# Joint product's tile kept for all batches and laid out by output rows; eight stores a batch; scores' half added up by block rows; another order at the end

## The chip, the cores and the metric

One Trainium2 chip, one core of it. The metric is the device time of one execution in microseconds; lower is better. Every time below is from the runs of the kernel before or from the profile of one of its executions. TensorE multiplies into eight accumulator banks, ScalarE and VectorE work on tiles, GpSimd does a few sums and issues the accumulating transfers, SyncE issues the other transfers.

## The reference, cut to what matters

32 graphs of 512 nodes with 512 features each, all in float32, pass through two layers:

```python
# layer 0
h   = max(layernorm(x), 0)
agg = einsum('bij,bjf->bif', adj, h) / max(sum(adj, -1), 1e-6)
x   = x + relu(concat([h, agg]) @ W.T)
# layer 1
h   = max(layernorm(x), 0)
q, k = split(h @ Wqk);  v = h @ Wv
agg = einsum('bij,bjd->bid', adj, k * mask)
w   = mask / sqrt(512) * einsum('bid,bid->bi', q, agg)
out = x + softmax(w, axis=nodes)[:, :, None] * v
```

Each graph ("batch") is independent of the others; the weights are shared.

## The kernel before

**Products.** Every 512x512 product is cut into 2x2 blocks of 256 and done with seven block products in place of eight: sums of blocks of the left and right factor are made beforehand (`left_sums`, `right_sums`: four additions each), and the seven results are added up into the four output blocks. The products run in the order 1, 2, 6, 5, 7, 3, 4 (`ORDER`).

**Layer 1 rewritten.** With M = Wq Wk^T, made once at the start, the row sums of q times agg are the row sums of (h M) times (adj (mask h)). So a batch needs a joint product of h with the pair M and Wv, called `tv` (index 0 of `which` is the scores' half h M, index 1 the values' half h Wv), and a product `u` of adj with mask h. `tv` applies the seven-product scheme twice, once over block rows and once more within: its blocks of 128 lie at seven "places", which must still be added up (`recombine`, seven additions for each half) before they are rows of the result. For each of the outer seven products it fills four banks, numbered n = 0 to 3, of two places each (the last of one), in the order 2, 1, 3, 0. ScalarE copies the banks of products 1, 6, 7 and 4 into the tile (`keep`), VectorE adds those of 2, 3 and 5 (`plus`, and the adds of `m_tv`). Products 1 and 6 continue in the same banks, so product 6 cannot begin before ScalarE has copied product 1's banks away; products 1 and 2 together occupy all eight banks.

**A period.** The main loop runs four stages of TensorE work in each period i, each a generator that is advanced step by step:

- `layer0_out(i)`, 14 steps: the output of layer 0 (`pp_o`, `pr_o`, `pq_o`),
- `layer1_tv(i - 1)`, 14 steps: the joint product (`ptv`),
- `layer1_u(i)`, 7 steps: adj times masked h (`pp_u` ...),
- `layer0_y(i + 1)`, 7 steps: h times the second half of W (`pp_y` ...).

What the other engines do is written out by hand as a `Plan`: `p.at(n, f, ...)` puts call f after step n of the stage. Each engine executes its instructions in that order, so an instruction that waits holds up all that come later on its engine. SyncE's transfers also go out in this order.

**What hangs on the joint product's tile.** In the stage after it VectorE adds up the scores' half, multiplies it by `U` and sums the rows (`dot`), then come the scores, their maximum over all nodes (GpSimd), the exponentials, the sum and the weights `sm`. In `layer0_out` of the following period ScalarE scales the four row groups of the values' half (`apply`, steps 2 to 5), GpSimd adds x to each half of them by an accumulating transfer from a DRAM copy (`add_x1`; the copy was written by `keep` of `FrontH1`), and SyncE stores them to the output (`store`, steps 9, 9, 11, 11: four transfers of 64 KB for each row group, 16 in all). Directly after that stage the next joint product begins, into the next tile of the same tag:

```python
t = big.tile([P, 4, 2, 7, P], F32, tag="tv", bufs=1, name=f"tv_{b}")
```

With one buffer, the first write into the new tile waits until everything that used the old one is done.

**Other names.** `FrontH1.write` normalises the rows of h for layer 1 (`h1m`, with `nmr` and `rstd` from VectorE's statistics) and writes them to DRAM (`dh1T`), from where they are read back in another order (`sh1T`) and turned; `mask` multiplies the same rows in place by the node mask on ScalarE, after that write has landed; `masked_sums` are the sums of `h1m` for `u`. `FrontA` does the same for adj (`a`, `daT`, `saT`), `FrontH` for layer 0's h (`n`, `dhT`, `shT`, `hT` in the tile `wide`). `inner_sums` are the second-level sums of `h1T` for the joint product. Reads of `a` for the batch after next are issued at steps 2 and 3 of the joint product, between the writes `dh1T`.

After the loop the last joint product runs alone (written into `wide`), with the end of batch 30 (`post`) and of batch 31 (`final`) beside and after it.

Of the kernel before, what the change touches and what calls it, by code (L numbers as in the profile page):

```python
# [16 lines left out]
P = 128  # L17
# [5 lines left out]
def kernel(  # L23
# [330 lines left out]
    class FrontH1:  # L354


        def __init__(self, b):
            self.b = b
            self.to = Turned("h1T", b)
            self.t = norm_tiles(f"1_{b}")  # L360
            self.x1 = dram.tile([2, P, 2, 2, H], F32, tag="dx1", name=f"dx1_{b}")
# [4 lines left out]
        def keep(self):  # L366
            for c in range(C):
                nc.sync.dma_start(
                    out=self.x1[c // 2][:, :, c % 2, :], in_=X[self.b][:, c, :].rearrange("p (a f) -> p a f", a=2)
                )  # L370
# [81 lines left out]
    def layer1_tv(b):  # L452


        if b + 1 < B:
            t = big.tile([P, 4, 2, 7, P], F32, tag="tv", bufs=1, name=f"tv_{b}")
        else:
            t = wide.rearrange("p s a (b f) -> p (s a b) f", f=P).rearrange("p (o a i) f -> p o a i f", o=4, a=2)
# [20 lines left out]
        def part(o, n):  # L479
            return t[:, o, :, 2 * n:min(2 * n + 2, 7), :].rearrange("p a b f -> p a (b f)")  # L480
# [29 lines left out]
    class Post:  # L510
# [12 lines left out]
        def recombine(self, i, blocks, which, on=None):  # L523
            def s(j):
                return TV[self.b][:, blocks, which, PLACE[j], :]

            o, x1, x2 = [(2, 1, 2), (1, 1, 6), (5, 1, 5), (3, 5, 3), (6, 1, 7), (7, 5, 7), (4, 6, 4)][i]
            add(s(o), s(x1), s(x2), on)

        def row(self, c, which):  # L530

            r, i = c // 2, c % 2
            return TV[self.b][:, 2 * r:2 * r + 2, which, 2 * i:2 * i + 2, :].rearrange("p a b f -> p a (b f)")

        def dot(self, c):
            v = self.row(c, 0)
            u = U[self.b][:, 2 * (c // 2):2 * (c // 2) + 2, c % 2, :]
            nc.vector.scalar_tensor_tensor(
                v, v, 1.0, u, op0=ALU.mult, op1=ALU.mult, accum_out=self.acc[:, c:c + 1]
            )  # L540
# [25 lines left out]

        def add_x1(self, h):
            nc.gpsimd.dma_start(
                out=TV[self.b][:, 2 * h:2 * h + 2, 1, 0:4, :].rearrange("p a i f -> p a (i f)"),
                in_=self.f1.x1[h].rearrange("p a i f -> p a (i f)"), accum_op=ALU.add,  # L570
            )

        def load_x1(self, h):
            self.n[h] = half_tile(f"x1_{self.b}_{h}")
            nc.sync.dma_start(out=self.n[h], in_=self.f1.x1[h].rearrange("p a i f -> p a (i f)"))

        def finish(self, c):

            x1 = self.n[c // 2].rearrange("p a (i f) -> p a i f", i=2)[:, :, c % 2, :]
            v = self.row(c, 1)  # L580
            nc.vector.scalar_tensor_tensor(v, v, self.sm[:, c:c + 1], x1, op0=ALU.mult, op1=ALU.add)

        def store(self, c):
            v = self.row(c, 1)
            for q, dst in enumerate(by_rows(out[self.b])):
                nc.sync.dma_start(  # L586
                    out=dst[:, c, :].rearrange("r (a f) -> r a f", a=2), in_=v[q * R:(q + 1) * R]
# [4 lines left out]
    w2R, hT = wide[:, 0:7], wide[:, 7:14]  # L592

# [245 lines left out]
    ends, middle, every = slice(0, 4, 3), slice(1, 3), slice(0, 4)  # L839
# [4 lines left out]
    with tc.manual_schedule(engines=engines):  # L844
        weights, mvR = start()
        post = None
        for i in range(B):
            more, last = i + 1 < B, i + 1 == B
            if i > 0:
# [8 lines left out]
                if i == 1:  # L858
# [9 lines left out]
                    p.at(6, FH[3].load, 0)  # L868
                    p.at(8, FH[3].load, 1)
                f1 = F1[i - 1]  # L870
                if post is not None:
                    for k in (5, 6):
                        p.at(0, post.recombine, k, every, 1)
                p.at(0, f1.turn, 0)
                p.at(1, f1.turn, 1)
                if post is not None:
                    for c in range(C):
                        p.at(2 + c, post.apply, c)
                        p.at([9, 9, 11, 11][c], post.store, c)
                    p.at(3, post.add_x1, 0)  # L880
                    p.at(5, post.add_x1, 1)
                for k in range(4):
# [33 lines left out]
                for c in range(C):  # L916
                    p.at([2, 3, 5, 6][c], f.write, c)
                    p.at(7 + c, f.mask, c)
                p.at(6, f.keep)
                for k in range(4):  # L920
                    p.at([9, 11, 12, 12][k], f.masked_sums, k)
# [16 lines left out]
                for k in range(7):  # L938
                    p.at(10 + k // 2, post.recombine, k, ends, 0)
# [16 lines left out]
            elif more:  # L956
                for k in range(7):
                    p.at(k // 4, post.recombine, k, middle, 0)
# [14 lines left out]
            else:  # L973
                p.at(0, f.turn, 0)
                p.at(1, f.turn, 1)
                for k in range(4):
                    p.at(2 + k // 2, f.sums, k)
                for k in range(4):
                    p.at(4 + k // 2, f.inner_sums, k, 0, 7)
# [5 lines left out]
            if more:  # L985
# [6 lines left out]
                if i > 0:  # L992
# [3 lines left out]
                    for k in range(5):  # L996
                        p.at(3 + (k + 1) // 2, post.recombine, k, every, 1)
# [26 lines left out]
        for k in range(7):  # L1024
            p.at(k // 2, post.recombine, k, every, 1, nc.gpsimd)
            p.at(1 + k // 2, post.recombine, k, middle, 0)
# [6 lines left out]
        for n, blocks in ((10, ends), (12, slice(1, 2))):  # L1033
            for k in range(7):
                p.at(n + k // 4, final.recombine, k, blocks, 0)
        p.at(12, post.shift)
        p.at(12, post.exponents)
        p.at(12, post.row_sum)
        p.at(13, post.weights)
# [4 lines left out]
        for k in range(7):  # L1044
            final.recombine(k, slice(2, 3), 0)
# [4 lines left out]
        for c in range(C):  # L1050
            post.apply(c)
        for k in range(3):
            final.recombine(k, every, 1)
# [41 lines left out]
```

## Time and profile before

| | |
|---|---|
| time, median of 3 runs | 2482.16 us (2480.3 to 2483.52) |
| span of the profiled execution | 2479.5 us |
| busy: TensorE, VectorE, ScalarE, GpSimd | 2306.0, 1938.8, 1081.8, 507.0 us |
| transfers | 463.71 MB, 468222 packets, mean 187 GB/s |
| stores to the output | 512 of 64 KB, 2.1 us from issue to landing |
| accumulating transfers | 62 of 512 KB, 8.0 us to landing |
| adds within the joint product's tile, of 128x256 | 0.42 us each (median) |

Busy time is a sum over the span; whether an engine sets the end is seen only from what waits for what, and where. The profile names a group of instructions by line, engine, operation and tile; `tv<-ptv` is a copy from a bank into the joint product's tile. After a number of us for idle time stands what ended it.

### The profile page before, as it was taken

The page shows a single profiled execution, that of the slowest core. Times are in us where ns is not written, and L with a number is a line of the kernel's source. Part 1 is how long each engine was busy: PE and PEld are TensorE (multiplying, and loading weights), DVE is VectorE, ACT ScalarE, POOL GpSimd, SP SyncE. Part 2 cuts the span into 40 slices and gives each one's busy share as a digit, 9 for nine tenths or more (in the row PEclk, how much of TensorE's full clock was granted, in tenths as well). Part 3 has the DMA queues.
Part 4 walks back from the last instruction along what each step waited for, and adds up shares of the span by engine and source line. Part 5 has one row for each costly group of instructions (what it writes and reads, how often), then busy time and mean ns, then how long its engine had stood idle before and what let it go on. Part 6 is the DMA issues. An engine that isn't in the chain of part 4 may idle for free.

```text
span 2479.5 us, 32904 instructions
## 1 busy us (share of the span) xinstructions
PE 2306.0 (93%) x10372; PEld 1997.3 (81%) x10372; DVE 1938.8 (78%) x3622; ACT 1081.8 (44%) x2031; POOL 507.0 (20%) x453
## 2 busy tenths in 40 slices
PE   7999999999999999999999999999999999999983
PEld 6788888887888888888888888888888888888872
DVE  6787778877778878788777788777788777798774
ACT  4354443454443444434444434544434544434331
POOL 0120222211222202222202222112222112222120
PEclk9999999999999999999999999999999999999996
DMA  9867687877787877877776878777877777777542
GB/s 221 230 187 190 176 217 181 201 191 186 192 207 175 208 189 179 210 187 188 200 187 176 218 178 203 194 193 180 218 176 204 192 194 184 207 181 189 129 111 51
DMA packets 468222, 463.71 MB, mean 187 GB/s; under 512 B 43312, under 2 KB 342320, under 8 KB 468048
## 3 DMA queue, kind: packets, MB, share of 16 engines
q1 hardware_dynamic: 451184, 429.10, 66.2%
q0 software_dynamic: 16864, 32.51, 7.5%
q8 instruction: 82, 1.34, 0.2%
q14 instruction: 92, 0.75, 0.1%
HBM read 293.93 MB, written 167.51 MB: 186 GB/s over the span
## 4 chain that ended last, share of the span: by engine, by line
PE 50%; DMA 17%; DVE 12%; SPq 8%; ACT 6%; issue 3%; POOL 3%; ACTq 0%; DVEq 0%; POOLq 0%
PE ptv L469 16%; PE pp_u L130 7%; SPq L586 7%; PE pp_y L130 7%; DMA tv<-dx 6%; PE pp_o L130 6%; DMA out_dram<-tv 4%; PE pq_u L130 4%; DVE tv L94 3%; PE pq_y L130 3%; PE pr_o L130 3%; ACT tv L100 2%; POOL y L97 2%; DVE h1T L97 2%; PE pr_y L130 2%
## 5 line engine op out<-in xcount | busy, mean ns | idle before, releaser
L469 PE MATMUL ptv<-mv,h1T 128*128 128x256 f32 x3136 | 736.7, 397 | 105.8 <-ACT tv L100 97.5
L469 PEld LDWEIGHTS ptv<-mv,h1T 128*128 128x128 f32 x3136 | 622.8, 200 | 214.5 <-ACT tv L100 109.6
L100 ACT ACTIVATE tv<-ptv 128x512 f32<-128x512 f32 x496 | 247.3, 549 | 300.6 <-DMA out_dram<-tv 204.2
L94 DVE TENSOR_TENSOR tv<-tv 128x256 f32<-128x256 f32 (+1 forms) x644 | 314.9, 512 | 8.5
L97 DVE TENSOR_TENSOR h1T<-h1T 128x512 f32<-128x512 f32 (+1 forms) x192 | 258.3, 1358 | 1.2
L130 PE MATMUL pp_u<-h1m,aT 128*128 128x256 f32 x1024 | 242.7, 380 | 8.2 <-DVE h1m L97 8.2
L130 PE MATMUL pp_y<-wide 128*128 128x256 f32 x1024 | 243.2, 381 | 0.0
L130 PE MATMUL pp_o<-y,aT 128*128 128x256 f32 x1024 | 243.1, 380 | 0.0
L130 PE MATMUL pp_o<-w,wide 128*128 128x256 f32 x992 | 236.4, 381 | 4.2 <-DMA w<-dw 4.2
L97 DVE TENSOR_TENSOR h1m<-h1m 128x512 f32<-128x512 f32 x128 | 88.8, 694 | 189.5 <-ACT h1m L382 188.4
L130 PEld LDWEIGHTS pp_u<-h1m,aT 128*128 128x128 f32 x1024 | 193.7, 190 | 38.1 <-issue 6.3
L130 PEld LDWEIGHTS pp_o<-y,aT 128*128 128x128 f32 x1024 | 195.4, 191 | 27.0
L130 PEld LDWEIGHTS pp_y<-wide 128*128 128x128 f32 x1024 | 195.4, 191 | 26.7
L130 PEld LDWEIGHTS pp_o<-w,wide 128*128 128x128 f32 x992 | 189.2, 191 | 31.4 <-issue 5.5
L94 DVE TENSOR_TENSOR tv<-ptv,tv 128x512 f32<-128x512 f32 x248 | 141.7, 612 | 89.6 <-ACT tv L100 69.2
L547 POOL PARTITION_ALL_REDUCE gtop<-top x32 | 22.2, 693 | 923.8 <-DVE top L544 923.8
L97 POOL TENSOR_TENSOR y<-y 128x512 f32<-128x512 f32 x124 | 192.8, 1555 | 16.8 <-DVE y L94 14.4
L100 ACT ACTIVATE o<-pp_o 128x512 f32<-128x512 f32 x96 | 57.3, 597 | 298.7 <-PE pp_o L130 298.7
L248 POOL TENSOR_TENSOR rstd<-rstd,mhalf 128x2 f32<-128x2 f32 (+1 forms) x96 | 78.4, 817 | 499.8 <-DVE rstd L247 499.8
L100 ACT ACTIVATE xu<-pp_u 128x512 f32<-128x512 f32 x128 | 76.4, 597 | 207.9 <-PE pp_u L130 202.3
L258 ACT ACTIVATE n<-n,nmr,rstd 128x512 f32<-128x512 f32 x120 | 88.3, 804 | 165.4 <-DVE nmr L252 144.0
L100 ACT ACTIVATE y<-pp_y 128x512 f32<-128x512 f32 x128 | 76.4, 597 | 169.0 <-PE pp_y L130 169.0
(113 smaller groups left out, 3464.3 us busy)
## 6 DMA issues: line engine op xcount, KB each, us to landing
w<-dw SPq DMA_DIRECT2D x217, 256.0 KB, 4.5
xu<-in_x_dram SPq DMA_DIRECT2D x128, 256.0 KB, 4.5
a<-in_adj_dram SPq DMA_DIRECT2D x256, 128.0 KB, 3.1
dh1T<-h1m SPq DMA_DIRECT2D x128, 256.0 KB, 3.1
dx<-xu SPq DMA_DIRECT2D x128, 256.0 KB, 3.5
sh1T<-dh1T SPq DMA_DIRECT2D x256, 128.0 KB, 4.4
shT<-dhT SPq DMA_DIRECT2D x248, 128.0 KB, 4.2
daT<-a SPq DMA_DIRECT2D x124, 256.0 KB, 4.5
```

Of the source, the lines that this page charges most:

```text
L94: (on or nc.vector).tensor_tensor(o, a, b, op=ALU.add)
L97: (on or nc.vector).tensor_tensor(o, a, b, op=ALU.subtract)
L100: nc.scalar.activation(o, i, AF.Copy)
L130: nc.tensor.matmul(p[:, rc, :], lt[:, LEFT[k], dk, ts(rc, P)], right[:, dk, :], start=first and n == 0, stop=True, skip_group_check=True,)
L248: nc.gpsimd.tensor_tensor(rstd[:, a:b], rstd[:, a:b], mhalf[:, a:b], op=ALU.pow)
L258: nc.scalar.activation(o, i, AF.Relu, scale=t[1][:, c:c + 1], bias=t[2][:, c:c + 1])
L469: nc.tensor.matmul(banks[n][:, :, ts(i, P)], left[:, LEFT[k], LEFT_IN[j], :], mvR[:, RIGHT[k], RIGHT[j], :, :], start=first and i == 0, st ...
L547: nc.gpsimd.partition_all_reduce(self.gtop, self.top, channels=P, reduce_op=ReduceOp.max)
L586: nc.sync.dma_start(out=dst[:, c, :].rearrange("r (a f) -> r a f", a=2), in_=v[q * R:(q + 1) * R])
```

## The change

- The joint product's tile `tv` is allocated once, for all batches, in place of a new tile for each batch under one buffer. Waits then go by the parts of the tile that an instruction touches.
- Its layout becomes [row half, scores or values, 14 positions, 128]: a pair of places of both blocks of a row half lie side by side, so that positions 0 to 7 of a half are its 256 output rows' values in order, and 8 to 13 are places that hold intermediate sums. Which places a bank covers stays.
- The output is stored by halves: 4 transfers for each of two halves, at steps 9 and 11, with 4 KB in a row on the tile's side. `keep` writes x in one transfer in place of four, and the accumulating transfers read and write 4 KB in a row.
- `recombine` takes a row half (0, 1, or both) in place of a list of blocks. The scores' half of row half 0 is added up at steps 12 and 13 (before: blocks 0 and 3 at steps 10 to 13), that of row half 1 at steps 0 and 1 of `u` (before: blocks 1 and 2).
- `mask` moves from steps 7, 8, 9, 10 to 7, 7, 8, 9, `masked_sums` from 9, 11, 12, 12 to 9, 10, 10, 11. In the second period two loads move from steps 6 and 8 to 9 and 10.
- At the end: batch 30's weights, scaling, accumulation and stores move beside the last joint product; the sums of `h1T` for it are made for the first two slots before the rest; the last batch is stored by halves, half of the transfers issued by ScalarE.

```diff
--- before.py
+++ after.py
@@ -358,16 +358,13 @@
             self.b = b
             self.to = Turned("h1T", b)
             self.t = norm_tiles(f"1_{b}")
-            self.x1 = dram.tile([2, P, 2, 2, H], F32, tag="dx1", name=f"dx1_{b}")
+            self.x1 = dram.tile([P, 2048], F32, tag="dx1", name=f"dx1_{b}")
 
...
         def keep(self):
-            for c in range(C):
-                nc.sync.dma_start(
-                    out=self.x1[c // 2][:, :, c % 2, :], in_=X[self.b][:, c, :].rearrange("p (a f) -> p a f", a=2)
-                )
+            nc.sync.dma_start(out=self.x1, in_=X[self.b].rearrange("p c f -> p (c f)"))
 
...
@@ -452,10 +449,11 @@
     def layer1_tv(b):
 
 
+
         if b + 1 < B:
-            t = big.tile([P, 4, 2, 7, P], F32, tag="tv", bufs=1, name=f"tv_{b}")
+            t = tv
         else:
-            t = wide.rearrange("p s a (b f) -> p (s a b) f", f=P).rearrange("p (o a i) f -> p o a i f", o=4, a=2)
+            t = wide.rearrange("p s a (b f) -> p (s a b) f", f=P).rearrange("p (r w i) f -> p r w i f", r=2, w=2)
         TV[b] = t
         left = H1T[b]
 
@@ -477,7 +475,8 @@
                 yield half
 
         def part(o, n):
-            return t[:, o, :, 2 * n:min(2 * n + 2, 7), :].rearrange("p a b f -> p a (b f)")
+            first = [0, 4, 8, 12][n] + (2 if n < 3 else 1) * (o % 2)
+            return t[:, o // 2, :, first:first + min(2, 7 - 2 * n), :].rearrange("p w b f -> p w (b f)")
 
...
@@ -520,20 +519,24 @@
                 setattr(self, n, small.tile([P, 1], F32, tag=n, name=f"{n}_{b}"))
             self.n = {}
 
-        def recombine(self, i, blocks, which, on=None):
+        def recombine(self, i, rows, which, on=None):
+
+
             def s(j):
-                return TV[self.b][:, blocks, which, PLACE[j], :]
+                p = PLACE[j]
+                first, step = (12, 1) if p == 6 else ([0, 4, 8][p // 2] + p % 2, 2)
+                t = TV[self.b][:, :, which, first:first + step + 1:step, :]
+                return t if rows is None else t[:, rows]
 
             o, x1, x2 = [(2, 1, 2), (1, 1, 6), (5, 1, 5), (3, 5, 3), (6, 1, 7), (7, 5, 7), (4, 6, 4)][i]
             add(s(o), s(x1), s(x2), on)
 
         def row(self, c, which):
 
-            r, i = c // 2, c % 2
-            return TV[self.b][:, 2 * r:2 * r + 2, which, 2 * i:2 * i + 2, :].rearrange("p a b f -> p a (b f)")
+            return TV[self.b][:, c // 2, which, 4 * (c % 2):4 * (c % 2) + 4, :].rearrange("p i f -> p (i f)")
 
         def dot(self, c):
-            v = self.row(c, 0)
+            v = self.row(c, 0).rearrange("p (a f) -> p a f", a=2)
             u = U[self.b][:, 2 * (c // 2):2 * (c // 2) + 2, c % 2, :]
             nc.vector.scalar_tensor_tensor(
                 v, v, 1.0, u, op0=ALU.mult, op1=ALU.mult, accum_out=self.acc[:, c:c + 1]
@@ -564,32 +567,35 @@
             v = self.row(c, 1)
             nc.scalar.activation(v, v, AF.Copy, scale=self.sm[:, c:c + 1])
 
+        def half(self, h):
+
+            return TV[self.b][:, h, 1, 0:8, :].rearrange("p i f -> p (i f)")
+
         def add_x1(self, h):
-            nc.gpsimd.dma_start(
-                out=TV[self.b][:, 2 * h:2 * h + 2, 1, 0:4, :].rearrange("p a i f -> p a (i f)"),
-                in_=self.f1.x1[h].rearrange("p a i f -> p a (i f)"), accum_op=ALU.add,
-            )
+            nc.gpsimd.dma_start(out=self.half(h), in_=self.f1.x1[:, ts(h, 1024)], accum_op=ALU.add)
 
         def load_x1(self, h):
             self.n[h] = half_tile(f"x1_{self.b}_{h}")
-            nc.sync.dma_start(out=self.n[h], in_=self.f1.x1[h].rearrange("p a i f -> p a (i f)"))
+            nc.sync.dma_start(out=self.n[h].rearrange("p c f -> p (c f)"), in_=self.f1.x1[:, ts(h, 1024)])
 
         def finish(self, c):
 
-            x1 = self.n[c // 2].rearrange("p a (i f) -> p a i f", i=2)[:, :, c % 2, :]
             v = self.row(c, 1)
-            nc.vector.scalar_tensor_tensor(v, v, self.sm[:, c:c + 1], x1, op0=ALU.mult, op1=ALU.add)
-
-        def store(self, c):
-            v = self.row(c, 1)
+            nc.vector.scalar_tensor_tensor(
+                v, v, self.sm[:, c:c + 1], self.n[c // 2][:, c % 2, :], op0=ALU.mult, op1=ALU.add
+            )
+
+        def store(self, h, also=None):
+            v = self.half(h).rearrange("p (c f) -> p c f", c=2)
             for q, dst in enumerate(by_rows(out[self.b])):
-                nc.sync.dma_start(
-                    out=dst[:, c, :].rearrange("r (a f) -> r a f", a=2), in_=v[q * R:(q + 1) * R]
+                (also if also is not None and q % 2 else nc.sync).dma_start(
+                    out=dst[:, 2 * h:2 * h + 2, :], in_=v[q * R:(q + 1) * R]
                 )
 
 
     wide = const.tile([P, 14, 2, H], F32, name="wide")
     w2R, hT = wide[:, 0:7], wide[:, 7:14]
+    tv = const.tile([P, 2, 2, 14, P], F32, name="tv")
 
     def weight_source(src):
         return src.rearrange("(k r) j -> k r j", r=R)
...
@@ -865,20 +870,21 @@
...
                     FH[3] = FrontH(3)
-                    p.at(6, FH[3].load, 0)
-                    p.at(8, FH[3].load, 1)
+                    p.at(9, FH[3].load, 0)
+                    p.at(10, FH[3].load, 1)
                 f1 = F1[i - 1]
                 if post is not None:
                     for k in (5, 6):
-                        p.at(0, post.recombine, k, every, 1)
+                        p.at(0, post.recombine, k, None, 1)
                 p.at(0, f1.turn, 0)
                 p.at(1, f1.turn, 1)
                 if post is not None:
                     for c in range(C):
                         p.at(2 + c, post.apply, c)
-                        p.at([9, 9, 11, 11][c], post.store, c)
                     p.at(3, post.add_x1, 0)
                     p.at(5, post.add_x1, 1)
+                    p.at(9, post.store, 0)
+                    p.at(11, post.store, 1)
                 for k in range(4):
                     p.at(2 + k, f1.sums, k)
                 for k in range(4):
@@ -915,10 +921,10 @@
                 p.at(3, shift, f.t, 2, 4)
                 for c in range(C):
                     p.at([2, 3, 5, 6][c], f.write, c)
-                    p.at(7 + c, f.mask, c)
+                    p.at([7, 7, 8, 9][c], f.mask, c)
                 p.at(6, f.keep)
                 for k in range(4):
-                    p.at([9, 11, 12, 12][k], f.masked_sums, k)
+                    p.at([9, 10, 10, 11][k], f.masked_sums, k)
                 if i + 2 < B:
                     fa = FA[i + 2] = FrontA(i + 2)
                     p.at(2 if i > 1 else 11, fa.load, 0)
@@ -936,7 +942,7 @@
                 p.at(6, exchanged.to.read, 0)
                 p.at(7, exchanged.to.read, 1)
                 for k in range(7):
-                    p.at(10 + k // 2, post.recombine, k, ends, 0)
+                    p.at(12 + k // 4, post.recombine, k, 0, 0)
                 run(layer1_tv(i - 1), 14, p)
 
 
@@ -955,7 +961,7 @@
                 p.at(3, FA[1].to.read, 1)
             elif more:
                 for k in range(7):
-                    p.at(k // 4, post.recombine, k, middle, 0)
+                    p.at(k // 4, post.recombine, k, 1, 0)
                 for c in range(C):
                     p.at(2 + c // 2, post.dot, c)
                 p.at(4, post.scores)
@@ -972,11 +978,14 @@
                         p.at(5, fa.degrees, 1)
             else:
                 p.at(0, f.turn, 0)
+                for k in range(3):
+                    p.at(1, f.inner_sums, k, 0, 2)
                 p.at(1, f.turn, 1)
                 for k in range(4):
                     p.at(2 + k // 2, f.sums, k)
+                p.at(4, f.inner_sums, 3, 0, 2)
                 for k in range(4):
-                    p.at(4 + k // 2, f.inner_sums, k, 0, 7)
+                    p.at(5 + k // 2, f.inner_sums, k, 2, 7)
             if more:
                 p.at(5, load_x, i + 1)
             run(layer1_u(i), 7, p)
@@ -994,7 +1003,7 @@
                     p.at(2, post.row_sum)
                     p.at(4, post.weights)
                     for k in range(5):
-                        p.at(3 + (k + 1) // 2, post.recombine, k, every, 1)
+                        p.at(3 + (k + 1) // 2, post.recombine, k, None, 1)
                 p.at(2, FA[i].factor)
                 if i == 0:
                     p.at(0, fh.write, 2)
@@ -1022,48 +1031,48 @@
         final = Post(B - 1, F1[B - 1])
         p = Plan()
         for k in range(7):
-            p.at(k // 2, post.recombine, k, every, 1, nc.gpsimd)
-            p.at(1 + k // 2, post.recombine, k, middle, 0)
+            p.at(k // 2, post.recombine, k, None, 1, nc.gpsimd)
+            p.at(1 + k // 2, post.recombine, k, 1, 0)
         for c in range(C):
             p.at(5 + c // 2, post.dot, c)
         p.at(7, post.scores)
         p.at(7, post.maximum)
         p.at(2, final.load_x1, 0)
         p.at(3, final.load_x1, 1)
-        for n, blocks in ((10, ends), (12, slice(1, 2))):
-            for k in range(7):
-                p.at(n + k // 4, final.recombine, k, blocks, 0)
-        p.at(12, post.shift)
-        p.at(12, post.exponents)
-        p.at(12, post.row_sum)
-        p.at(13, post.weights)
+        for k in range(7):
+            p.at(12, final.recombine, k, 0, 0)
+        p.at(8, post.shift)
+        p.at(8, post.exponents)
+        p.at(9, post.row_sum)
+        p.at(10, post.weights)
+        for c in range(C):
+            p.at(10 + c, post.apply, c)
+        p.at(11, post.add_x1, 0)
+        p.at(13, post.add_x1, 1)
+        p.at(13, post.store, 0)
+        p.at(13, post.store, 1)
         p.at(13, final.dot, 0)
         p.at(13, final.dot, 1)
         run(layer1_tv(B - 1), 14, p)
 
         for k in range(7):
-            final.recombine(k, slice(2, 3), 0)
+            final.recombine(k, 1, 0)
         final.dot(2)
         final.dot(3)
         final.scores()
         final.maximum()
-        for c in range(C):
-            post.apply(c)
         for k in range(3):
-            final.recombine(k, every, 1)
+            final.recombine(k, None, 1)
         final.shift()
         final.exponents()
         final.row_sum()
-        for h in range(2):
-            post.add_x1(h)
         for k in range(3, 7):
-            final.recombine(k, every, 1)
+            final.recombine(k, None, 1)
         final.weights()
         for c in range(C):
             final.finish(c)
-            final.store(c)
-        for c in range(C):
-            post.store(c)
+            if c % 2:
+                final.store(c // 2, nc.scalar)
 
 
 # ---- launch: one core; inputs and outputs as the reference has them ----
```

More of the change, by code (lines that the diff above doesn't have):

```diff
@@ L836, in start @@
         return [right_sums(outer)[k] for k in range(4)] + [right_sums(inner)[k] for k in range(4)], mv
-    ends, middle, every = slice(0, 4, 3), slice(1, 3), slice(0, 4)
     engines = {
```

## Prediction

> **What bounds the kernel now.** I read the waits first (who waited for whom, in total over the span), then one batch in the timeline, then stretches of that batch with clock and busy time, then VectorE's timeline, because a second limit must lie behind the first.
>
> ```profile
> ACT tv L100 <- DMA out_dram<-tv: 204.2, 30, 15.3
> ...
> PEld ptv L469 <- ACT tv L100: 109.6, 30, 4.5
> ...
> PE ptv L469 <- ACT tv L100: 97.5, 30, 4.1
> ...
> PE pp_u L130 <- DVE h1m L97: 8.2, 8, 1.5
> ```
>
> TensorE (93% busy) has one large wait: 97.5 us, in 30 of 32 batches, in the joint product, for ScalarE's copies into `tv`; ScalarE in turn waits for stores that read `tv`. One batch shows how:
>
> ```profile
> 1246.10 10.32 SPq L586 DMA_DIRECT2D out_dram<-tv  x16
> ...
> 1248.87 6.21 PE L469 MATMUL ptv<-mv,h1T 128*128 128x256 f32 x28
> ...
> 1258.43 1.85 ACT L100 ACTIVATE tv<-ptv 128x512 f32<-128x512 f32 x4 [7.23 <-DMA out_dram<-tv]
> 1259.06 1.29 DVE L94 TENSOR_TENSOR tv<-ptv,tv 128x512 f32<-128x512 f32 x2 [3.71 <-ACT tv L100]
> ...
> 1259.08 17.06 PE L469 MATMUL ptv<-mv,h1T 128*128 128x256 f32 x70 [4.01 <-ACT tv L100]
> ```
>
> The sixteen stores take 10.3 us of SyncE's issue, start only when the accumulating DMA has landed (1246.10) and end with a landing at about 1258. TensorE can fill eight banks (28 matmuls) without a copy, then stands for 4 us. The wait costs more than itself:
>
> ```profile
> 1255.20:1259.00 3.80, 0.00 (x0) 0.00 (x0) 0.15 (x1) 0.57 (x2) 0.70 (x1) 1.00 0.69 211
> 1259.00:1262.00 3.00, 2.92 (x9) 2.39 (x10) 2.94 (x6) 3.00 (x7) 0.00 (x0) 0.64 0.46 170
> 1262.00:1265.00 3.00, 3.00 (x13) 2.52 (x12) 0.48 (x1) 2.64 (x6) 0.00 (x0) 0.79 0.85 260
> ```
>
> The second number after the stretch is TensorE's busy time, the third from the end the granted clock: it falls to 0.64 and 0.79 after the stand, so about 1.7 us more are lost. The first joint product, which has no store before it, shows the stage without both; later ones begin 75.02 us apart, (2372.29 - 196.79)/29:
>
> ```profile
> 127.10 21.32 PE L469 MATMUL ptv<-mv,h1T 128*128 128x256 f32 x98
> ...
> 196.79 6.21 PE L469 MATMUL ptv<-mv,h1T 128*128 128x256 f32 x28
> ```
>
> With 21.15 for it and 24.17, 12.09 and 12.09 for the three other stages (starts of `pp_o`, `pp_u`, `pp_y` in the timeline) a period without waits is 69.5 us: 5.5 us lie open. VectorE is next, from one period's adds of `m_tv` to the following batch's `nmr`:
>
> ```profile
> 1272.13 2.23 DVE L94 TENSOR_TENSOR tv<-tv,m_tv 128x512 f32<-128x512 f32 x4 [2.95 <-ACT tv L100]
> ...
> 1290.15 1.41 DVE L97 TENSOR_TENSOR wide<-wide 128x512 f32<-128x512 f32 x2
> ...
> 1331.06 0.13 DVE L252 SCALAR_TENSOR_TENSOR nmr<-mv,rstd 128x2 f32<-128x2 f32 x1
> ```
>
> 58.9 us, of which VectorE idles about 3 (1.50 for `sh1T`, 1.18 for GpSimd, 0.29); in the other periods this stretch is 58.2 to 59.4 us, wherever TensorE stands. It is serial work, not waiting.
>
> **What the Trainium skill says.** "TensorE: Matmul & The Clock Gate" (Part 1: The HAM clock gate) says that an idle window of about 3.4 us halves the array's clock, and a busy one restores it; the trace agrees (0.64 and 0.79 after 4 us), and after the last such stand of 1.8 us the 70 matmuls took 15.38 us, not 17.06. So waits under about 2 us should cost only themselves. "SBUF — State Buffer" (Who interferes with whom) says that a VectorE tensor-tensor with two SBUF inputs and a GpSimd operation block each other; here an `h1T` sum of 128x512 beside GpSimd's `y` sums takes up to 1.76 us in the timeline, the like `h1m` sum 0.69. The change keeps this overlap, so I leave the 58.4 as it is. "DMA: Bandwidth & Descriptors" (Issuing engines are not separate DMA queues) says a second issuing engine saves only issue time; issue time is what the end of this kernel consists of.
>
> **The change, part by part.**
>
> 1. One tile for all batches. Before, the first copy of a batch waited for everything that used the old tile: all 16 stores. In the changed program's list of waits the first copy (places 4, 5, positions 8 to 11) waits for TensorE alone, the second (positions 4 to 7) for the four stores of half 0 and their accumulating DMA, and the copies of product 7 for those of half 1. Four stores from 1246.10 at 0.64 each are issued by 1248.7; with the 2.1 us landing of a 64 KB store, up to 1 us more for 128 KB, they are done at 1250.8 to 1252. ScalarE is busy with `n` until 1251.2 anyway, and TensorE needs these copies at 1255.1. The wait falls away: 4.0 + 1.7 us a period.
> 2. Eight stores for sixteen, one `keep` for four: SyncE's issue falls by about 5 us and 2 us a period. No later wait hangs on it except the `dhT` writes behind the stores, which come 5 us earlier, as TensorE does: neutral.
> 3. The recombining adds: 14 of 0.42 us before, 14 of the same 256 elements after, at 12-13 instead of 10-13: no time. `masked_sums` now stand ahead of them: the third ends 3.6 us after the adds of `m_tv` begin (2.23 + 2 x 0.69) instead of 7.7. That removes the 8.2 us of `pp_u`.
> 4. `mask` one step earlier. It waits in ScalarE's queue until the write of the same rows has landed (22.3 us over 28 waits before). Behind it now stand the copies of product 7, behind those the adds of `m_tv`. From `nmr`: normalise 1.05, first to third `dh1T` issue 5.45 (1261.01 to 1266.46, eight loads of `a` between), landing and release 3.4 (3.1 median, 4.16 in this batch), then mask 0.72, copies 1.1, mask 0.72, copies 0.85 and 0.1: 13.4 us to the adds.
> 5. So VectorE closes a loop: 58.4 + 13.4 = 71.8, with a little more waiting for `sh1T` 72.0 us. That is over TensorE's 69.5, and it sets the period. Where it shows: the third `hT` sum ends about 19.0 us after the adds begin (1272.13 to 1291.2); `nmr` at 6.3 puts the adds at 19.7 after the joint product's start and the sum at 38.7, while the third product of `y` wants it at 21.15 + 12.09 + 3.45 = 36.7. TensorE should stand about 2 us in `pp_y`, too short for the clock to fall.
> 6. The gain inside: 27 periods by 75.0 - 72.0 = 3.0: 81 us. The last two periods have no loads of `a` between the `dh1T` writes and fewer statistics; there 69.6, 2 x 5.4 = 11. The last stalled joint product (1.8 us) gives 2.
> 7. The end. `inner_sums` of the first slots before the rest: the last joint product now waits 6.20 us for `h1T`, and its 96 matmuls take 23.93 instead of 20.7; about 2 us may stay: 7. The last rows are finished at 2456.2; then 32 stores take until 2476.5 to issue. Batch 30's now go out beside the last matmuls, and of the final eight the last four lie on two queues: 2456.2 + 2 x 0.62, and 3.0 to the end of the span as before (2476.5 to 2479.5), 0.6 more for the larger store: 2461, so 18.
>
> Sum 81 + 11 + 2 + 7 + 18 = 119: 2482 - 119 = 2363; taken as 2361, as `mask` may land sooner than its median wait suggests.
>
> **The rivals.**
>
> A. TensorE alone bounds it. If landings and masks are quicker (the loop under 69.5 needs 11 us from `nmr` to the adds), 29 x 5.5 = 160, with the end's 27 it is 187: 2295. For it: the first period took 69.7. Against it: that period consumed a lead, as `nmr` came 2.5 us after the start of the joint product there, and 6 in all later ones.
>
> B. The store stays on the path in part: the second copy now waits at the head of ScalarE's queue, and four others stand behind it. If half 0 lands 4 us later than I work out, 2 us of stand remain and period 74: 29 + 27 = 56, 2426. Against: 4 us of room in the batch shown, and stores start at most 0.5 us later in others.
>
> C. Not faster, or slower. If masks block ScalarE so that the copies for product 4 come late, TensorE stands inside the joint product too. To eat the end's gain, the period must reach 76, 4 us over my loop; at 76.4 it is 2495. Against: the longest wait of `mask` was 1.8 us, and landings of `dh1T` are 3.1 in the median.
>
> **How the numbers follow.** VectorE's loop 0.70, A 0.17, B 0.09, C 0.04. Time 2361. The loop's uncertain terms are the landing (3.1 to 4.2) and the waits for `sh1T` (0.3 to 2): periods of 71 to 73.2, or 2332 to 2395; the range goes from 2300, near A, to 2405, towards B. Faster takes all but C and a part of nothing else: 0.95; same 0.02; slower 0.03.
>
> **What would show it.** Right: no wait of ScalarE for `out_dram` of any size, no clock under 0.95 in mid-span, joint products of 21.2 us, about 72 us between them, and a new wait of `pp_y` for VectorE's `wide` of 1 to 2.5 us a batch; the span ends 5 us after the last `finish`. Wrong: periods of 69.5 (A); a wait of `ptv` for ScalarE that stays (B, C); the adds of `m_tv` much earlier than 19 us after the joint product's start, which would say that step 4 is mis-sized.

## The result, and the profile after

The changed kernel takes 2360.03 us in the median of four runs (2356.24 to 2362.98); the kernel before, on the same chip, 2481.23 (2472.81 to 2483.52). The ratio is 0.9517 [0.949, 0.9543]: 121 us less. The forecast was 2361. The profiled spans are 2354.3 and 2479.5 us, the mean granted clock 0.996 and 0.972.

The list of waits of the changed kernel (engine, what it waited to do, and for whom; us in total, times, longest) no longer holds the two large ones of before: ScalarE's copies into `tv` do not wait for `out_dram`, and TensorE does not wait in `ptv` for ScalarE. What it does hold:

```profile
ACT e L556 <- DVE ntop L553: 92.4, 31, 8.5
...
ACT h1m L379 <- DMA dh1T<-h1m: 60.6, 55, 2.5
ACT n L258 <- DMA out_dram<-tv: 55.0, 8, 7.2
...
PE pp_y L130 <- DVE wide L97: 32.6, 28, 1.7
...
DVE h1T L285 <- DMA sh1T<-dh1T: 28.0, 19, 5.7
...
PE ptv L467 <- DVE xu L442: 14.2, 26, 1.0
```

One line still names `out_dram`, for ScalarE's `n`. In each of its eight cases VectorE's `nmr`, which `n` reads, ended only 0.03 to 0.04 us before `n` began, so `n` could not have begun earlier, stores or no stores.

TensorE's largest wait in the loop is now the one that was forecast, `pp_y` for VectorE's `wide`: 1.16 us in each of 28 batches. A small one was not forecast: `ptv` waits 0.5 us a batch for VectorE to read the last bank of `pp_o`. The joint product in stretches of one batch (length, then the busy times of TensorE, its weight loads, VectorE, ScalarE and GpSimd, granted clock, DMA share, GB/s):

```profile
1199.60:1205.00 5.40, 5.32 (x25) 4.36 (x23) 5.08 (x10) 4.64 (x8) 0.61 (x2) 1.00 0.91 294
1205.00:1210.00 5.00, 4.97 (x23) 4.42 (x24) 4.89 (x12) 4.01 (x8) 0.86 (x2) 1.00 0.37 116
1210.00:1215.00 5.00, 5.00 (x25) 4.41 (x24) 1.00 (x2) 3.74 (x7) 0.00 (x0) 1.00 0.93 266
```

Before, the corresponding stretches held a stand of 3.8 us and clocks of 0.64 and 0.79; here TensorE is busy nearly throughout, at 1.00, and its clock is 1.00 in each stretch of 50 us from 50 to 2300. One period of the changed kernel in the timeline (start, length, engine, idle before and what ended it):

```profile
1199.58 21.69 PE L467 MATMUL ptv<-mv,h1T 128*128 128x256 f32 x98
...
1205.83 0.13 DVE L252 SCALAR_TENSOR_TENSOR nmr<-mv,rstd 128x2 f32<-128x2 f32 x1
...
1216.35 0.72 ACT L379 ACTIVATE h1m<-h1m,mraw 128x512 f32<-128x512 f32 x1 [2.47 <-DMA dh1T<-h1m]
...
1219.45 2.23 DVE L94 TENSOR_TENSOR tv<-tv,m_tv 128x512 f32<-128x512 f32 x4 [5.59 <-ACT tv L100]
...
1237.58 1.41 DVE L97 TENSOR_TENSOR wide<-wide 128x512 f32<-128x512 f32 x2
1238.91 0.15 DVE L553 TENSOR_SCALAR ntop<-gtop 128x1 f32<-128x1 f32 x1
...
1239.09 0.30 ACT L556 ACTIVATE e<-w,ntop 128x4 f32<-128x4 f32 x1 [3.04 <-DVE ntop L553]
1239.29 1.32 ACT L343 ACTIVATE a<-a,rdeg 128x512 f32<-128x512 f32 x2
...
1242.14 4.38 SPq L212 DMA_DIRECT2D sh1T<-dh1T  x8
...
1252.38 1.30 DVE L285 STREAM_TRANSPOSE h1T<-sh1T 128x512 f32<-128x512 f32 x2 [1.42 <-DMA sh1T<-dh1T]
...
1278.18 0.13 DVE L252 SCALAR_TENSOR_TENSOR nmr<-mv,rstd 128x2 f32<-128x2 f32 x1
```

From `nmr` to the adds of `m_tv` it is 13.62 us, from there to the next `nmr` 58.73: the loop of the prediction, 72.35 in this batch. The starts of the joint products 2 and 30 give the mean of 28 periods, 71.75 us; before it was 75.01:

```profile
195.02 21.48 PE L467 MATMUL ptv<-mv,h1T 128*128 128x256 f32 x98
...
2204.06 21.32 PE L467 MATMUL ptv<-mv,h1T 128*128 128x256 f32 x98
```

The end:

```profile
2306.79 0.59 PE L467 MATMUL ptv<-mv,h1T 128*128 128x256 f32 x2
2307.69 2.43 PE L467 MATMUL ptv<-mv,h1T 128*128 128x256 f32 x10 [0.30 <-DVE h1T L97]
2312.47 19.10 PE L467 MATMUL ptv<-mv,h1T 128*128 128x256 f32 x86 [2.35 <-DVE h1T L97]
...
2347.59 2.62 SPq L591 DMA_DIRECT2D out_dram<-wide  x4
```

The last matmul ends at 2331.57, 22.7 us ahead of the span's end; before it was 41.2. Of the 125.2 us between the spans, 28 x 3.26 = 91.3 come from the periods, 7.7 from the last one, 1.8 from the start, and 24.4 from the last joint product on.

### The profile page after: what moved, and what is told of

The parts are those of the page before. It is cut to its first block, busy times and chain, and to the rows that moved or that the text cites. A ratio compares the mean times of both kernels' runs of the same rounds, so it can differ in the third digit from the quotient of the medians.

```text
span 2354.3 us, 32391 instructions
## 1 busy us (share of the span) xinstructions
PE 2263.0 (96%) x10372; PEld 1966.8 (84%) x10372; DVE 1946.8 (83%) x3619; ACT 1078.4 (46%) x2031; POOL 495.3 (21%) x453
## 4 chain that ended last, share of the span: by engine, by line
DVE 37%; DMA 23%; PE 21%; ACT 10%; issue 3%; SPq 3%; POOL 2%; DVEq 0%; ACTq 0%; POOLq 0%
DVE tv L94 12%; DMA dh1T<-h1m 6%; PE pp_o L130 5%; PE pp_y L130 5%; DVE st L242 4%; ACT tv L100 4%; DMA tv<-dx 3%; DMA shT<-dhT 3%; DVE tv L541 3%; DMA sh1T<-dh1T 3%; PE ptv L467 3%; ACT h1m L258 3%; PE pq_y L130 3%; DMA daT<-a 3%; DVE h1T L97 3%
## 5 line engine op out<-in xcount | busy, mean ns | idle before, releaser
L467 PE MATMUL ptv<-mv,h1T 128*128 128x256 f32 x3136 | 690.5, 380 | 17.1 <-DVE xu L442 14.2
L467 PEld LDWEIGHTS ptv<-mv,h1T 128*128 128x128 f32 x3136 | 593.9, 190 | 108.5 <-DVE xu L442 26.0
L130 PE MATMUL pp_y<-wide 128*128 128x256 f32 x1024 | 245.8, 383 | 32.6 <-DVE wide L97 32.6
L100 ACT ACTIVATE tv<-ptv 128x512 f32<-128x512 f32 x496 | 241.3, 537 | 62.2 <-PE ptv L467 61.2
L97 DVE TENSOR_TENSOR h1T<-h1T 128x512 f32<-128x512 f32 (+2 forms) x195 | 259.6, 1344 | 1.2
L94 DVE TENSOR_TENSOR tv<-tv,m_tv 128x512 f32<-128x512 f32 x124 | 69.2, 620 | 141.9 <-ACT tv L100 138.9
```

The lines of the kernel that those rows point to most:

```text
L94: (on or nc.vector).tensor_tensor(o, a, b, op=ALU.add)
L97: (on or nc.vector).tensor_tensor(o, a, b, op=ALU.subtract)
L100: nc.scalar.activation(o, i, AF.Copy)
L130: nc.tensor.matmul(p[:, rc, :], lt[:, LEFT[k], dk, ts(rc, P)], right[:, dk, :], start=first and n == 0, stop=True, skip_group_check=True,)
L467: nc.tensor.matmul(banks[n][:, :, ts(i, P)], left[:, LEFT[k], LEFT_IN[j], :], mvR[:, RIGHT[k], RIGHT[j], :, :], start=first and i == 0, st ...
```

## The experiments

Two theories stood after the result. **Loop**: the period is set by VectorE's work and the masks in a ring, so whatever removes the stand in the joint product gives the same time. **Tile**: the kept tile itself brings the gain. All runs below are against the kernel before on the same chip, which took 2478 to 2483 us in the median.

### Which part removes the stand

A new tile for each batch again, the eight stores left:

```diff
-            t = tv
+            t = big.tile([P, 2, 2, 14, P], F32, tag="tv", bufs=1, name=f"tv_{b}")
```

> The changed kernel with a new tile for each batch again (one buffer), its layout and its eight stores kept. Loop theory (VectorE's loop of about 71.7 us sets the period; a wait for stores costs only where copies come later than about 6.2 us after the joint product's start): the eight stores are issued 1.4 us after that start and land by 4.2, so the copies end about 6.1, TensorE has no stand for them, ScalarE is free when nmr comes at 6.7: 2360 us within 8, period 71.7. Tile theory (the kept tile is what took the wait away): stand and half clock come back, 2430 to 2480 us.

Measured 2361.9, ratio 0.9515 [0.9499, 0.9531]: no loss. Next sixteen stores of one row group each (at steps 9, 9, 11, 11) with the kept tile:

```diff
-                    p.at(9, post.store, 0)
-                    p.at(11, post.store, 1)
+                    for c in range(C):
+                        p.at([9, 9, 11, 11][c], post.store_rows, c)
```

> The changed kernel with its kept tile, but sixteen stores of 64 KB, four for each row group, at steps 9, 9, 11, 11. Loop theory: at about 0.4 us of issue each the burst ends 3.6 us after the joint product's start, dhT after it by 5.8, before the first dh1T at 7.1: 2360 to 2370 us. If a store of 64 KB takes 0.6 us of issue as before the change, dh1T starts 2.4 us later and the period grows by as much: 2430 us. Rival (the number of stores does not matter once the tile is kept): 2360.

Measured 2371.98, 0.9555 [0.9531, 0.9579]: 12 us lost, though not as a stand in the joint product (TensorE's wait for ScalarE there is 1.1 us in all); TensorE's wait in `pp_y` is 38.9 us in place of 32.6. Both undone together:

> The changed kernel with both undone: a new tile for each batch and sixteen stores, in the new layout, with the new order of masks and sums. Loop theory: the last landing is 6 to 10 us after the joint product's start, copies end at 8 to 12, the normalising follows them: period 73 to 76 us, 2395 to 2480 us. Tile theory: as e1.

Measured 2408.48, 0.971 [0.9682, 0.9738]: 48 us lost, far more than the two losses (2 and 12) added. The list of waits has ScalarE's old wait for the stores again, but hardly TensorE's stand:

```profile
ACT tv L100 <- DMA out_dram<-tv: 83.2, 25, 11.7
...
PE pp_y L130 <- DVE wide L97: 43.0, 24, 2.0
...
PE pp_o L130 <- DMA w<-dw: 15.6, 7, 2.7
...
PE ptv L467 <- ACT tv L100: 9.9, 17, 1.7
```

This run has neither the kept tile nor the eight stores, and yet TensorE waits 9.9 us for ScalarE's copies, where before it was 97.5. What it keeps is the rest of the change, the layout above all: with 2 KB in a row in the tile a store of 64 KB takes 0.42 us of SyncE's issue, not 0.59, and the last of the sixteen lands 6.0 us after the joint product's start, not 8.8 (medians). TensorE fills its eight banks in 6.2 us, so at 6.0 little of a stand is left. The 48 us are lost further on. ScalarE's copies are late, and behind them in its queue so is the normalising of `h1m`: from `nmr` to the adds of `m_tv` it is 14.8 us in the median, not 13.2, and TensorE waits longer in `pp_y`, and in `pp_o` for `w`. Against this loss either the kept tile or the eight stores is enough, and the second adds little. The reverse, the kernel before with nothing changed but one tile for all batches, in its old layout:

```diff
-            t = big.tile([P, 4, 2, 7, P], F32, tag="tv", bufs=1, name=f"tv_{b}")
+            t = tv
```

> The kernel before with one thing changed: its tile, in its old layout, allocated once for all batches; sixteen stores, old steps, old end. The second copy then waits for the second group of four stores, which lands about 5.1 us after the joint product's start: no stand over 1 us, clock near full. Loop theory: dhT now ends 9.7 us after that start and holds up the first dh1T by 2.4 us, the masks stand one step later, which saves 1.4: period 72.7, 2481 - 29 x 2.3 = 2414 us, with a wait of pp_u for h1m of about 3 us a batch. Tile theory (the rest of the change brings only its end, 27 us): 2385 us.

Measured 2440.18, 0.9825 [0.9804, 0.9846]: 41 us gained, less than either theory said. The waits tell why:

```profile
PE pp_u L130 <- DVE h1m L97: 51.3, 25, 2.5
...
PE pp_o L130 <- DMA w<-dw: 20.1, 10, 2.9
...
PE ptv L469 <- ACT tv L100: 5.5, 10, 0.9
```

The stand in `ptv` is gone (97.5 to 5.5), but the masked sums in their old place, behind the recombining adds, now hold TensorE up for 51.3 us in `u`, where they had held it for 8.2; and late loads of `w` cost 20.1. In no run with the new order does TensorE wait for the masked sums, nor in the next one, which has the masks at their old steps; that speaks for the order of the sums and the adds as the cure, though these were not moved alone.

### The loop: masks, and VectorE's work at three places

Masks at 7, 8, 9, 10, as they were before, with the rest of the new order kept:

```diff
-                    p.at([7, 7, 8, 9][c], f.mask, c)
+                    p.at([7, 8, 9, 10][c], f.mask, c)
```

> The changed kernel with the masks one step later, as before the change (7, 8, 9, 10), masked_sums kept at 9, 10, 10, 11. Loop theory: only the third mask, which waits for its write to land, still stands ahead of two copies; the adds of m_tv begin about 1.4 us earlier, the period falls from 71.7 to 70.3: 2360 - 27 x 1.4 = 2322 us. Rival (TensorE and its small waits alone set the period, the place of mask is without effect): 2360 us. Rival of the change's order (later masks delay masked_sums and pp_u): 2365 to 2380 us.

Measured 2313.53, 0.932 [0.9299, 0.934]: 46 us faster than the changed kernel. From `nmr` to the adds of `m_tv` it is 11.7 us in the median in place of 13.2, and the period falls by as much, to 70.3 us. Within the new order the earlier masks were a loss. Two of them later still:

```diff
-                    p.at([7, 7, 8, 9][c], f.mask, c)
+                    p.at([7, 8, 10, 10][c], f.mask, c)
```

> The changed kernel with the third and fourth mask behind the last copies of product 7 (7, 8, 10, 10). Loop theory: the adds of m_tv no longer wait for dh1T to land, they begin 16.2 to 16.9 us after the joint product's start instead of 19.3; the loop is 68.9, under TensorE's 69.5, so TensorE sets the period: 69.6 to 70.1 us, 2300 to 2316 us, and the wait of pp_y for wide falls from 32.6 us to under 5. Rival (place of mask without effect): 2360 us.

Measured 2333.24, 0.9398 [0.9373, 0.9423]: a miss. The wait of `pp_y` is gone, but `nmr` to the adds takes anything from 10.1 to 14.2 us (12.3 in the median), and another wait has come:

```profile
PE pp_o L130 <- DMA w<-dw: 34.9, 18, 3.0
```

SyncE's queue in this run shows where it comes from:

```profile
1170.23 4.44 SPq L204 DMA_DIRECT2D n<-in_x_dram  x8
1175.12 5.18 SPq L409 DMA_DIRECT2D w<-dw  x3
1180.39 4.79 SPq L212 DMA_DIRECT2D shT<-dhT  x8
1185.28 0.40 SPq L409 DMA_DIRECT2D w<-dw  x1
```

The last load of `w` is issued behind eight reads of `shT`, and lands 7.8 us later; TensorE wants it at 1192.0 and starts with it at 1193.2. The reads cannot be all of it: in the changed kernel the load stands behind them too and lands in time. The other difference is its place against GpSimd's accumulating transfers. Here the first of these was issued 0.9 us ahead of the load:

```profile
1184.40 1.96 POOL L575 DMA_DIRECT2D tv<-dx  x2
```

In the changed kernel it was 0.2 us in this batch, and the load landed 4.2 us after its issue:

```profile
1189.68 1.96 POOL L575 DMA_DIRECT2D tv<-dx  x2
...
1189.89 0.39 SPq L409 DMA_DIRECT2D w<-dw  x1
```

Over all batches: where the load went out ahead of that transfer or at most 0.6 us behind it, it landed after 2.7 to 6.0 us in the changed kernel (all 30 batches) and after 4.9 in the median here (13 batches, 4.4 to 9.0); where it went out later, after 6.8 to 10.5 us (the other 17 here). To test whether the wait for `w` is what holds this run up, the same masks with the reads of `shT` behind that load:

```diff
-                    p.at(5, th.to.read, 0)
-                    p.at(6, th.to.read, 1)
+                    p.at(7, th.to.read, 0)
+                    p.at(8, th.to.read, 1)
```

> The masks at steps 7, 8, 10, 10 as in the run that lost time in pp_o to a wait for w, and now the reads of shT at steps 7 and 8 of that stage in place of 5 and 6, so that SyncE issues the last load of w ahead of the eight of shT, some 5 us earlier. If that wait alone kept the masks' order from its gain: no wait of pp_o for w, o stages of 24.2 us, clock at 1.00, a period of 69.5, and 2298 to 2310. If the loop only finds the next limit (shT late for its turn, or another wait of VectorE), the time stays at 2325 to 2340.

Measured 2302.13, 0.9276 [0.9259, 0.9293]: as expected of the wait for `w` as the only cause, and the fastest kernel of this study. No wait for `w` is left; `nmr` to the adds takes 10.1 us, every `o` from the second period on 24.17, and the period is 70.0. The load, now ahead of the reads and in 29 of 30 batches not over 0.6 us behind the accumulating transfer, lands after 2.6 to 3.5 us in these; which of the two it must be ahead of was not tried by itself. Alone, that edit should do nothing to the changed kernel:

> The changed kernel with only the reads of shT moved from steps 5 and 6 of the stage of o to 7 and 8, behind the last load of w. The loop through VectorE sets the period of the changed kernel, and TensorE waits for w only once in it, so nothing is won: 2355 to 2365, with the wait of pp_y for wide left as it is. If the loads of w were what held the changed kernel too, the period would fall here as it did with the other masks: 2300 to 2330.

Measured 2363.71, 0.9532 [0.951, 0.9554]: nothing.

Then VectorE's work. Two of the values' half recombining adds, in the stage of `y`, left out:

```diff
-                    for k in range(5):
+                    for k in range(3):
                         p.at(3 + (k + 1) // 2, post.recombine, k, None, 1)
```

> The changed kernel without two of the seven adds of the values' half (the fourth and fifth, 0.68 and 0.65 us each on VectorE), in all batches that the loop adds up; their output blocks are left out. Loop theory: VectorE's stretch falls by 1.3 us, the period from 71.7 to 70.4: 2360 - 28 x 1.3 = 2324 us. Rival (TensorE and its small waits, or landings of transfers, set the period and VectorE has room): 2355 to 2360 us.

Measured 2361.14, 0.9515 [0.9494, 0.9536]: no gain from 1.3 us less work a batch. VectorE's timeline of one batch:

```profile
1237.32 0.15 DVE L553 TENSOR_SCALAR ntop<-gtop 128x1 f32<-128x1 f32 x1
...
1248.73 1.31 DVE L285 STREAM_TRANSPOSE h1T<-sh1T 128x512 f32<-128x512 f32 x2 [2.00 <-DMA sh1T<-dh1T]
1250.99 1.30 DVE L285 STREAM_TRANSPOSE h1T<-sh1T 128x512 f32<-128x512 f32 x2 [0.96 <-DMA sh1T<-dh1T]
```

It waits 2.96 us for `sh1T`, where the batch of the changed kernel waits 1.42: the work left out has become waiting. From `ntop` to the second turn of `h1T` it is 13.7 us here (1237.32 to 1250.99) and 13.5 in the changed kernel (1238.91 to 1252.38). The work that was cut lies between these two.

So work ahead of `ntop` should count. The four `hT` sums (2.75 us) were moved from `u` into the joint product, where VectorE idles:

```diff
                     p.at(3, th.turn, 1)
+                    for k in range(4):
+                        p.at(5 + k // 2, th.sums, k)
...
-                for k in range(4):
-                    p.at(5 + k // 2, th.sums, k)
```

> The four hT sums (2.75 us of VectorE's work) move from the stage of u, where they stand inside the stretch from the adds of m_tv to nmr, into the joint product, at its steps 5 and 6, where VectorE waits for masks and copies anyway; nothing is left out. If the place of the work in the loop counts (the adds of m_tv, then VectorE's work up to the third hT sum, then TensorE's y), TensorE's wait of pp_y for wide goes away, the period falls to TensorE's 69.5 to 70.2, and the time is 28 x 1.5 to 2.0 lower: 2305 to 2320. If VectorE's work counts nowhere, because it only waits longer for sh1T afterwards, as when two adds were left out of the stage of y, the time stays within 2350 to 2362.

Measured 2409.58, 0.9711 [0.9686, 0.9735]: both theories missed, by far. The wait of `pp_y` went away, but in `o`:

```profile
PE pp_o L130 <- DMA w<-dw: 55.5, 20, 3.7
...
PE pp_o L130 <- ACT n L258: 30.3, 10, 3.8
```

In 29 of 30 batches the last load of `w` is now issued more than 0.6 us behind the first accumulating transfer, and it lands 9.8 us after its issue in the median. Why the move of the sums shifts the two was not traced, nor the wait for ScalarE's `n`, which is gone in the next run.

With the reads of `shT` behind the last load of `w`:

> The four hT sums in the joint product, as in the run that came out at 2410 with 55 us of waits for w, and now the reads of shT behind the last load of w; the masks stay at 7, 7, 8, 9. If the 2.75 us of VectorE's work taken out of the loop were hidden there only by the late loads of w, they show now: no wait of pp_y for wide, o stages of 24.2 us, periods of 69.5 to 70.5, and 2302 to 2330. If the sums in the joint product cost as much as they save (they delay the masked sums or nmr), 2345 or more.

Measured 2313.76, 0.9334 [0.9313, 0.9355]. The same four sums in the same new place cost 50 us with the one order of SyncE and gain 46 with the other; waits for `w` in `o` fall to 11.3 us. The period is 70.2. From the adds of `m_tv` to the next `nmr` it is 56.9 us in the median, in the changed kernel 58.6, and VectorE has slack again:

```profile
DVE h1T L285 <- DMA sh1T<-dh1T: 88.6, 58, 4.7
```

### The end

The old order of the end: all sums of `h1T` together, batch 30's weights, scaling and accumulation after the last matmul, both batches' stores on SyncE:

```diff
-        p.at(8, post.shift)
+        p.at(12, post.shift)
...
-                final.store(c // 2, nc.scalar)
+                final.store(c // 2)
+        for h in range(2):
+            post.store(h)
```

> The changed kernel with the end's order undone: sums of h1T for the last joint product in the old order, batch 30's scaling and stores after the last batch, all stores on SyncE (but eight and eight of them, not sixteen and sixteen). Working of the prediction: the h1T order is worth 7 us, the stores 8 x 0.6 more at the end and four on one queue 1.2 more: 2360 + 7 + 6 = 2373 us. If the end is worth what the prediction gives it in all (25 us, with half of the stores gone): up to 2385 us. Rival (the end hides behind the last rows): 2360 us.

Measured 2372.66, 0.9559 [0.9539, 0.958]: the new end is worth 12.6 us in the changed kernel. The last joint product here waits 7.20 us for `h1T`.

## Why the prediction was right, step by step

- **Step 1, the stand falls away: right, but put down to one cause where there are more.** The joint product runs at full clock. Yet the kept tile was not needed for it: with eight stores a new tile gives 2361.9, and even with sixteen in the new layout TensorE stands for 9.9 us only.
- **Step 2, eight stores "neutral": wrong.** With a new tile for each batch they are worth 47 us (2408.5 to 2361.9). The prediction reckoned with the old issue time of 0.64 us for a store; in the trace of after it is 0.43, and the eight take 3.3 us of issue a batch in the median, the sixteen of before 9.5. With a new tile and eight stores the last one lands 3.6 us after the joint product's start (4.8 at most), so a wait for every store ends before TensorE needs the banks. As the kept tile alone prevents this loss too, the sum was not touched by it.
- **Step 3, the masked sums: mis-sized.** It counted 8.2 us of `pp_u` (and read the third sum's end at 7.7 us after the adds began; in the trace it is 7.2, at 1279.28). The kernel before with only the kept tile shows 51.3 us: the stand had hidden it. The sum came out since the 3.0 us a period of step 6 assumed these sums in time.
- **Step 4, 13.4 us from `nmr` to the adds: right** (13.2 in the median, 12.7 to 14.8). It did not ask whether another order of masks would be better; with later masks, and `w` in time, it is 10.1.
- **Step 5, the loop, 71.8 to 72.0 us: right in size** (71.75), and `pp_y` waits for `wide` as forecast, 1.2 us in place of 2. Of the difference 0.5 us is the wait of `ptv` for VectorE's reading of a bank, which the prediction did not have, and 0.4 a reading: the third `hT` sum of its batch ended at 1290.83, not at 1291.2. "It is serial work, not waiting" was wrong for a part. Between `ntop` and the turn of `h1T` the traces show a second way round: ScalarE's exponent waits for `ntop` (92.4 us in all), behind it three scalings of `a`, their writes to `daT`, and the eight reads of `sh1T` (3.2 us from `ntop` to the first, 10.2 from there to the second turn). The Trainium skill, "Perfetto Trace Analysis" (Tensor Engine Instruction), calls ScalarE's execution queue strictly first in, first out; the trace agrees: the factors for the scalings were ready at 1237.08, but they start at 1239.29, right after the exponent at 1239.09. VectorE's work there is about as long (1.4 us of waiting in that batch), and so shortening it alone brings nothing. That the cut in `y` is swallowed and the cut ahead of `ntop` counts is measured; that the exponent is the link was read from the traces (its waits are 90.5 us with the two adds left out, 16.4 with the `hT` sums moved and `shT` later) and was not tried by moving the exponent alone.
- **Step 6: 81 + 11 + 2 = 94, measured 91.3 + 7.7 = 99.** Over 28 periods each gains 3.26 in place of 3.0 over 27; what comes after them gains 7.7 in place of 13, since one period at the end, not two, is at TensorE's 69.5.
- **Step 7, the end, 7 + 18 = 25: 24.4 by the spans.** The last joint product now stands 2.65 us for `h1T` in place of 6.20, and the tail is 18.5 us shorter. Undoing the new order there costs only 12.6 us: from the start of the last joint product to the end of the span it is 71.9 us before, 61.2 with the old order and 47.5 after, so some 10 us of the 24 are not from the order but from what that run keeps, probably the larger and fewer stores (that split was not tried).
- **The rivals.** A, TensorE alone at 69.5: not in this kernel, but the last period, without loads of `a`, took 69.5. B, a store on the path: no such wait is left. C: no.
- **Luck.** The loop, its size and its place were right, and these carry most of the sum. That 2361 and 2360.0 agree to 1 us is luck: in the profiled spans the parts differ by 5 us inside, 2 at the start and 1 at the end, and which parts of the change matter was only half known.

## What to carry to other kernels

Where two edits each remove the same wait, undo them singly and together: one alone shows little lost and hides that the other is enough. Then look at which wait came back: here the time did, the stand of TensorE did not. A wait removed uncovers those it hid, here 8 us of late sums that became 51 and an order of loads that turned a gain of 46 us into a loss of 50; so judge an edit again after the next limit is cured. When cutting work from an engine in a loop changes nothing, look for the branch that runs beside it (here ScalarE's queue and a DMA) and cut ahead of the fork.

## What was unexpected of the hardware

A store took 0.59 us of SyncE's issue in the median for 64 KB with 1 KB in a row on the tile's side, 0.42 for 64 KB with 2 KB in a row and 0.43 for 128 KB with 4 KB: the time went with the number and shape of the transfers, not with their bytes. The shape is not all: in the runs of 2302.13 and 2313.76 us the same stores of 128 KB took 0.32.

The same load of `w` (256 KB) landed after 2.7 to 6.0 us in all 30 batches of the changed kernel, where it went out ahead of a 512 KB accumulating transfer of GpSimd or at most 0.6 us behind it. Issued further behind, it took 6.8 to 10.5 us in 17 batches with the masks at 7, 8, 10, 10, and 5.7 to 10.9 in 29 with the `hT` sums moved, but only 3.6 to 7.5 in seven batches of the kernel before. So it is a tendency of these runs; no run moved the accumulating transfer alone.
